# Eight layers on one core: the third attention's head outputs by channel, the fourth attention as a pipeline, and pieces of work moved between stages

## The chip, the core and the metric

The kernel runs on one core of one Trainium2 chip. Time is device microseconds of one execution, the median of several runs. A core has five engines with an instruction stream each, which meet through semaphores: PE (TensorE: matmuls and transposes; its weight loads are listed apart as PEld), DVE (VectorE), ACT (ScalarE), POOL (GpSimd) and SP (SyncE, which here issues DMAs). Results of PE land in PSUM and are read from there by DVE or ACT; everything else lies in SBUF. An engine executes its own instructions in order.

## The reference, cut to what matters

Sixteen batches (16 x 128 tokens x 256 channels, float32) go through eight layers: four cross-attentions, each followed by a feed-forward. Each layer works on a layernorm of x and adds its result to x.

```python
x = x + L0_xattn(ln(x), ctx, pos, ...)     # 32 heads of 8, rotary positions
x = x + L0_ffn(ln(x), ...)                 # product-key experts
x = x + L1_xattn(ln(x), ctx, mask, ...)    # 16 heads of 128
x = x + L1_ffn(ln(x), ...)                 # 7 routed experts (top 2) and a shared one
x = x + L2_xattn(ln(x), ctx, ...)
x = x + L2_ffn(ln(x), ...)                 # ternary weights
x = x + L3_xattn(ln(x), ctx, ...)
x = x + L3_ffn(ln(x), ...)                 # weights and activations rounded to fp8 by blocks of 32
```

The two attentions that the change rebuilds:

```python
def L2_xattn(x, y, ...):                    # 16 heads of 16; y has 128 tokens
    y_main, y_dca = y[:, :112], y[:, 112:]
    q     = _ln(x @ Wq + bq) * qn_w + qn_b          # each head by itself
    k     = _ln(y_main @ Wk + bk) * kn_w + kn_b;            v     = y_main @ Wv + bv
    k_dca = _ln(y_dca @ Wkd + bkd) * kn_dca_w + kn_dca_b;   v_dca = y_dca @ Wvd + bvd
    o = softmax(q k^T * 0.25) v + softmax(q k_dca^T * 0.25) v_dca     # two softmaxes
    return o @ Wo + bo

def L3_xattn(x, y, ...):                    # 16 heads of 128
    q, k, v = rmsnorm(x @ Wq, gq), rmsnorm(y @ Wk, gk), y @ Wv
    return (softmax(q k^T / sqrt(128)) v) @ Wo
```

## The kernel before, in words

`run` (L1610) goes through the plan of seven weight blocks and the eight stages in turn; weights of a later stage are loaded on SP while earlier ones compute. x stays in SBUF, one 128x256 tile for each batch. All matmuls are float32, and one matmul is two passes (two instructions) on PE in the trace. The order in which a stage's Python code emits work is the base of each engine's order; a scheduler may move an instruction within its queue, `high_priority` draws it forward, and `issue_after(i)` keeps a piece of work behind instruction i.

**Start.** `setup` loads x of two batches on SP, and positions, constants, context and `rows` (biases spread over the partitions) on ACT's queue; `run` then issues the first weights and the other x on SP. In `l0_attn` the work is `inputs` (layernorm and transposes of four batches), `front`, `turn`, `start` (scores and exponentials, `l0_terms`), `l0_heads`, `l0_norm`, `l0_out`; `inputs(1)` is held behind the last rotary multiply of `front(1)`. `l0_heads` packs four heads in 32-column tiles of PE (L356).

**First feed-forward** (`l0_ffn`). In batch b, behind the weights of each half, the `units` of batch b+1 are computed, two pieces for each half.

**Second feed-forward** (`l1_ffn`). Tokens are sorted into blocks of 128 rows for each expert; a loop over t does the stages of the blocks (fetch, unit, gate, down) as a pipeline. `shared(bs)` is the shared expert for a group of batches, a generator whose pieces are drawn forward by `next`. After the loop come `l2_inputs(0)`, `shared(groups[2])` and further `l2_inputs`. `l2_inputs(g)` gathers two routed results for each of two batches (`combine`, by indirect DMA on POOL's queue, then two DVE multiply-adds each, L1007), and makes the layernorm and transposes of them.

**Third attention** (`l2_attn`, L1062). For a batch, `front` makes q, k and v by matmuls, adds biases (DVE L1099, L1101), squares (ACT), reduces and takes the inverse root (DVE), then POOL multiplies by it (L1108), by the norm's weight (L1110), adds its bias (L1111), and writes v twice into `vx`, times the mask of main tokens and of the 16 others (L1115), beside columns of ones for the sums. `turn` transposes q and k (PE), copies them (ACT L1127) and spreads k over a block diagonal `kbd` (POOL L1130). For each half c of the heads: `l2_terms` makes the scores (PE L1173) in one PSUM buffer of two banks, the two maxima and subtractions (DVE L1182, L1184; 112 and 16 keys), and the exponential (ACT L1187). `l2_heads` transposes the exponentials (PE L184 `pT`), copies them (ACT L1198) and multiplies by `vx` in 64-column tiles, so that po has rows of outputs and sums for each head (PE L1202); ACT copies po to `u` (L1207). `l2_norm` transposes `u` back to tokens by channels (`pu`), takes the reciprocals of 16 sums for each token (DVE L1215) and multiplies (two L1217). `l2_out` transposes the sum of both softmaxes (L1227 `poT`), copies it (ACT L1229), adds `bo` to x on POOL (L1230), multiplies by Wo (PE L1233) and adds to x (DVE L1234). The loop keeps scores half a batch ahead, `turn` two batches ahead, `front` three.

**Fourth attention** (`l3_attn`). Batches go in groups of two. `project(g)` is a generator in six pieces: keys (PE `pk` L1386, POOL `kt` L1398, transposes `pkT`), queries (PE `pq` L1426, DVE `q` L1429), sums of squares (`pssq` L1433) and scales. For each batch and each r of four sets of four heads: scores S (PE L1472), maximum and scale (DVE L1474, L1475), four exponentials with sums (ACT L1479), reciprocal (DVE L1483), normalisation (POOL L1484), then a piece of the next group's `project`, then transposes `pT`, copy `eT` (DVE L1488), `po` (PE L1490), copy `oT` (DVE or ACT in turns), and `py` (PE L1498). One step's work is emitted whole before the next step's. With a group, one sixth of the last weights is rounded (`quantize`, 32 blocks).

**Last feed-forward** (`l3_ffn`). `quantize` rounds 1024 columns: maximum, scale, reciprocal and multiply on DVE, two adds (L1520, L1521) on the engine that the caller names (DVE for weights, POOL for x and h), and a multiply on POOL (L1522).

Of the kernel before, what the change touches and what calls it, by code (L numbers as in the profile page):

```python
# [34 lines left out]
for _name, _w in (  # L35
    ("bout0", 256), ("br", 8), ("gbias", 8), ("bq2", 256), ("bo2", 256), ("qn_w", 16), ("qn_b", 16),
    ("bkv_main", 512), ("bkv_dca", 512), ("kn_w", 16), ("kn_b", 16), ("knd_w", 16), ("knd_b", 16),
):
    ROWS[_name] = (_n, _w)
    _n += _w  # L40
# [12 lines left out]
class Net:  # L53
# [15 lines left out]
    def setup(self):  # L69
# [15 lines left out]
        nc.scalar.dma_start(out=self.rows, in_=a["rows"][0:NALL].partition_broadcast(P))  # L85
        nc.scalar.dma_start(out=self.ctxT[:, 2:B], in_=ctxT[:, 2:B])
        self.gains = cp.tile([P, 2], F32, tag="gains", name="gains")
        nc.scalar.dma_start(out=self.gains, in_=a["gains"])
# [129 lines left out]
    def l0_attn(self, w):  # L218
# [6 lines left out]
        with ExitStack() as es:  # L225
# [20 lines left out]
            def front(b):  # L246
# [15 lines left out]
                for k in range(2):  # L262
                    last = nc.vector.tensor_tensor(
                        by_head(t)[:, :, :, k], src[:, :, :, 1 - k], bc(self.sinT[:, b, :, k], 1, 64), ALU.mult
                    )
# [4 lines left out]
                return last  # L270
# [22 lines left out]
            last = front(1)  # L293
# [3 lines left out]
            with tc.issue_after(last.ins):  # L297
                inputs(1)
# [20 lines left out]
    def l0_terms(self, sp, kp, sc, b, c, qkT, kbd):  # L319
# [12 lines left out]
        for k in range(2):  # L332
# [3 lines left out]
            nc.vector.tensor_tensor(E[:, two], S[:, two], bc(mx, 3, P), ALU.subtract)  # L336
# [47 lines left out]
    def l0_ffn(self, w):  # L384
# [6 lines left out]
        with ExitStack() as es:  # L391
# [45 lines left out]
            sh = [units(0, q) for q in range(4)]  # L437
            for b in range(self.nb):
                more = b + 1 < self.nb
                nxt, after = [], None  # L440
                for half in range(2):
# [10 lines left out]
                    if more:  # L452
# [387 lines left out]
    def l1_ffn(self, w, after, ctx):  # L840
# [5 lines left out]
        with ExitStack() as es:  # L846
# [130 lines left out]
            rounding = self.ternary(sp, mm, after[:, 2048:])  # L977
            for t in range(NBLK + 2):
# [9 lines left out]
                if t > 10:  # L988
                    next(rounding, None)
            for _ in rounding:  # L990
                pass
            for g, bs in enumerate(groups[2:]):
                self.l2_inputs(g, tr)
# [18 lines left out]
    def l2_setup(self, ctx, w):  # L1012
# [10 lines left out]
        nc.gpsimd.tensor_copy(cd[:, :, 112:P], self.ctxT[:, :, 112:P])  # L1023

        bqk = op.tile([P, 32, 16], F32, tag="bqk", name="bqk")
        bv = op.tile([P, 256], F32, tag="bv", name="bv")
        nw = op.tile([P, 2, 16], F32, tag="nw", name="nw")
        nbi = op.tile([P, 2, 16], F32, tag="nbi", name="nbi")
        flat = bqk.rearrange("p h d -> p (h d)")
        for t, main, dca, skip, n in (  # L1030
            (flat[:, 256:512], "bkv_main", "bkv_dca", 0, 256), (bv, "bkv_main", "bkv_dca", 256, 256),
            (nw[:, 1, :], "kn_w", "knd_w", 0, 16), (nbi[:, 1, :], "kn_b", "knd_b", 0, 16),
        ):
            for name, part in ((main, slice(0, 112)), (dca, slice(112, P))):
                at = ROWS[name][0] + skip
                nc.scalar.dma_start(
                    out=t[part], in_=self.a["rows"][at : at + n].partition_broadcast(part.stop - part.start)
                )
        nc.vector.tensor_copy(flat[:, 0:256], self.row("bq2"))
        nc.vector.tensor_copy(nw[:, 0, :], self.row("qn_w"))  # L1040
        nc.vector.tensor_copy(nbi[:, 0, :], self.row("qn_b"))
# [7 lines left out]
        self.l2_const = cd, flat, bv, nw, nbi  # L1049
# [12 lines left out]
    def l2_attn(self, w):  # L1062
# [4 lines left out]
        Wo = w[:, 1536:2048].rearrange("p (c n) -> p c n", c=2)  # L1067
        with ExitStack() as es:
# [4 lines left out]
            tr = es.enter_context(tc.tile_pool(name="l2tr", bufs=2, space=PSUM))  # L1073
            pvp = es.enter_context(tc.tile_pool(name="l2pv", bufs=2, space=PSUM))
            cd, flat, bv, nw, nbi = self.l2_const

            vp = es.enter_context(tc.tile_pool(name="l2v", bufs=1))
            vx = [vp.tile([P, 16, 2, 32], F32, tag=f"vx{k}", name=f"vx{k}") for k in range(3)]
            for t in vx:
                for s in range(2):  # L1080
                    nc.scalar.copy(t[:, :, s, :], self.consts[:, 16 + s : 17 + s].unsqueeze(2).to_broadcast([P, 16, 32]))
# [708 lines left out]
```

## Time and profile before

| | us |
|---|---|
| runs (3) | 2538.73, 2539.52, 2540.11; median 2539.52 |
| profiled execution | 2537.55, its span 2535.8 |

| stretch of the span (us) | stage | length | PE busy | DVE busy | ACT busy | POOL busy |
|---|---|---|---|---|---|---|
| 13 to 291 | first attention | 278 | 247.6 | 206.8 | 172.0 | 68.2 |
| 296 to 714 | first feed-forward | 418 | 398.7 | 349.2 | 220.8 | 166.1 |
| 714 to 1147 | second attention | 433 | 409.6 | 239.8 | 168.3 | 109.2 |
| 1155 to 1365 | second feed-forward | 210 | 197.2 | 135.2 | 57.6 | 35.8 |
| 1365 to 1395 | third attention up to its first scores | 30 | 17.0 | 21.3 | 6.3 | 21.4 |
| 1395 to 1643 | third attention | 248 | 209.4 | 168.1 | 110.0 | 107.6 |
| 1650 to 1777 | third feed-forward | 127 | 127.0 | 32.7 | 17.1 | 3.6 |
| 1778 to 2317 | fourth attention | 539 | 509.3 | 336.1 | 285.2 | 148.9 |
| 2321 to 2536 | last feed-forward | 215 | 192.8 | 153.5 | 44.1 | 136.9 |

The second table is the view of busy time by stretch. A stretch whose length is close to PE's busy time is bound by PE; where no engine comes near the length, the time lies in waits of one engine for another. Rows of instructions, where they are shown below, give line, engine and operation, out<-in with shapes, the count, then busy time and the mean ns of one, then the idle time before them and who ended it.

### The profile page before, as it was taken

How to read it: one execution, taken by the hardware profiler on the slowest of the kernel's cores; microseconds unless marked ns; L12 is line 12 of the kernel's file. 1: busy time of each engine (PE TensorE's matmuls, PEld its weight loads, DVE VectorE, ACT ScalarE, POOL GpSimd, SP SyncE). 2: the span in 40 equal slices, each digit the busy share in tenths (PEclk: the TensorE clock that was granted, in tenths of full speed). 3: DMA queues.
4: the chain of work that ended last, by engine and by line, in shares of the span. 5: the costliest groups of instructions: out<-in, count | busy, mean ns of one | idle time of the engine just before them, and what ended most of it. 6: DMA issues, size and time to landing. Idle time of an engine off the chain costs nothing.

```text
span 2535.8 us, 37146 instructions
## 1 busy us (share of the span) xinstructions
PE 2320.0 (91%) x13628; PEld 1708.8 (67%) x13628; DVE 1665.5 (66%) x3884; ACT 1088.4 (43%) x2848; POOL 811.8 (32%) x736
## 2 busy tenths in 40 slices
PE   6999799999999999998997888799899999998798
PEld 3555589899977777775874455455576666665465
DVE  7777588888855555555666776532556666657964
ACT  4666555454524333441331444411555555554121
POOL 3222234343412222231007554200212222224765
PEclk8999899999999999999997899999999999999899
DMA  9000200000020000002224000000100000000000
GB/s 368 17 2 1 84 1 1 1 1 1 3 118 8 12 10 10 14 13 86 79 67 158 1 1 1 1 1 0 68 1 1 1 1 1 1 1 1 7 13 15
DMA packets 29845, 74.18 MB, mean 29 GB/s; under 512 B 6864, under 2 KB 21464, under 8 KB 24032
## 3 DMA queue, kind: packets, MB, share of 16 engines
q1 hardware_dynamic: 24768, 60.48, 6.4%
q0 software_dynamic: 3072, 8.39, 0.9%
q10 hardware_dynamic: 1824, 2.94, 0.3%
q8 instruction: 109, 1.79, 0.3%
q14 instruction: 72, 0.59, 0.1%
HBM read 45.84 MB, written 25.95 MB: 28 GB/s over the span
## 4 chain that ended last, share of the span: by engine, by line
PE 65%; DVE 21%; ACT 6%; POOL 4%; issue 4%; DMA 1%; POOLq 0%; ACTq 0%; DVEq 0%; SPq 0%
PE pT L184 5%; DVE g L519 5%; PE r L533 4%; PE py L669 4%; PE pt L608 4%; PE py L1498 3%; PE p L1315 3%; PE po L653 2%; PE fh L427 2%; PE fy L546 2%; PE py L1589 2%; PE pq L1426 2%; PE py L1323 2%; PE pg L1576 2%; PE pu L1576 2%
## 5 line engine op out<-in xcount | busy, mean ns | idle before, releaser
L184 PE MATMUL pT<-ident,E 128*128 128x128 f32 x1280 | 203.2, 285 | 45.1 <-POOL E L1484 11.9
L184 PEld LDWEIGHTS pT<-ident,E 128*128 128x128 f32 x1280 | 147.1, 145 | 100.9 <-issue 26.5
L509 POOL TENSOR_TENSOR g<-sim 128x1024 f32<-128x1024 f32 x64 | 140.5, 2215 | 217.6 <-ACT sim L474 183.0
L519 DVE SCALAR_TENSOR_TENSOR g<-g,th 128x1024 f32<-128x1024 f32 x128 | 194.6, 1580 | 0.0
L515 ACT ACTIVATE g<-sim 128x128 f32<-128x128 f32 x512 | 159.8, 391 | 33.5 <-PE r L533 32.9
L634 ACT ACTIVATE E<-E,mx 128x128 f32<-128x128 f32 x256 | 99.5, 390 | 160.0 <-DVE mx L631 138.6
L1479 ACT ACTIVATE E<-S,mx,sc 128x128 f32<-128x128 f32 x256 | 113.9, 458 | 83.3 <-DVE mx L1475 82.3
L1484 POOL TENSOR_TENSOR E<-E,rs 128x512 f32<-128x512 f32 x64 | 66.6, 1041 | 236.2 <-DVE rs L1483 106.0
L533 PE MATMUL r<-ident,g 128*128 128x128 f32 x1024 | 123.4, 275 | 18.6 <-DVE g L519 18.5
L669 PE MATMUL py<-w_w_l,oT 128*128 128x256 f32 x512 | 128.2, 383 | 5.3 <-DVE x L671 3.7
L533 PEld LDWEIGHTS r<-ident,g 128*128 128x128 f32 x1024 | 114.4, 142 | 26.4 <-DVE g L519 17.5
L1426 PE MATMUL pq<-xnT,w_w_l 128*128 128x256 f32 x512 | 126.7, 384 | 3.5 <-ACT sqk L1392 1.7
L639 POOL TENSOR_TENSOR E<-E,rs 128x512 f32<-128x512 f32 x64 | 66.6, 1041 | 194.7 <-DVE rs L638 144.8
L1498 PE MATMUL py<-w_w_l,oT 128*128 128x256 f32 x512 | 125.8, 387 | 3.1 <-DVE oT L65 2.9
L608 PE MATMUL pt<-xnT,w_w_l 128*128 128x256 f32 x512 | 121.1, 382 | 0.0
L427 PE MATMUL fh<-xnT,w_w_f 128*128 128x128 f32 x1024 | 121.0, 277 | 0.0
L669 PEld LDWEIGHTS py<-w_w_l,oT 128*128 128x128 f32 x512 | 93.9, 190 | 39.7 <-issue 20.4
L546 PE MATMUL fy<-w_w_f,wT 128*128 128x256 f32 x512 | 118.3, 379 | 0.0
L427 PEld LDWEIGHTS fh<-xnT,w_w_f 128*128 128x128 f32 x1024 | 116.7, 192 | 1.9
L1426 PEld LDWEIGHTS pq<-xnT,w_w_l 128*128 128x128 f32 x512 | 94.7, 191 | 28.6 <-issue 12.3
L1498 PEld LDWEIGHTS py<-w_w_l,oT 128*128 128x128 f32 x512 | 92.8, 190 | 29.1 <-DVE oT L65 11.6
L608 PEld LDWEIGHTS pt<-xnT,w_w_l 128*128 128x128 f32 x512 | 95.0, 192 | 15.2 <-issue 2.5
(403 smaller groups left out, 5561.6 us busy)
## 6 DMA issues: line engine op xcount, KB each, us to landing
w_w_f<-in_w_f SPq DMA_DIRECT2D x14, 1024.0 KB, 11.8
sent<-zero SPq DMA_DIRECT2D x14, 1024.0 KB, 20.6
w_w_l<-in_w_l SPq DMA_DIRECT2D x14, 1024.0 KB, 10.3
xb<-sent SPq DMA_DIRECT2D x38, 128.0 KB, 2.0
back<-yb SPq DMA_DIRECT2D x38, 128.0 KB, 1.8
x<-in_x SPq DMA_DIRECT2D x16, 128.0 KB, 2.9
out<-x SPq DMA_DIRECT2D x16, 128.0 KB, 1.7
ctx<-in_ctx ACTq DMA_DIRECT2D x1, 1024.0 KB, 8.0
```

The costliest lines, as they stand in the source:

```text
L184: self.nc.tensor.transpose(ps[:, i, :], src(i), self.ident)
L427: nc.tensor.matmul(ps[:, k, :], down[:, c, a * P : (a + 1) * P], xT[:, c, :], start=c == 0, stop=c == 1)
L509: nc.gpsimd.tensor_tensor(g, bc(sim[:, 2 * h, 8 * half : 8 * half + 8], 2, P), bc(sim[:, 2 * h + 1, :], 1, 8), ALU.add)
L515: nc.scalar.activation(g[:, k, :], sim[:, 2 * h + 1, :], AF.Identity, bias=sim[:, 2 * h, a : a + 1])
L519: nc.vector.scalar_tensor_tensor(gf, gf, th[:, h : h + 1], gf, ALU.is_ge, ALU.mult)
L533: nc.tensor.matmul(ps[:, k, :], G[h][:, 4 * q + k, :], self.ident, start=h == 0, stop=h == 3, is_transpose=True)
L546: self.nc.tensor.matmul(py, wT[:, k, :], up[:, a, :], start=a == 0, stop=a == 15)
L608: nc.tensor.matmul(ps[:, k], A[:, h + k, c, :], xT[:, c, :], start=c == 0, stop=c == 1)
L669: nc.tensor.matmul(pys[b], oT[:, j, :], Wo[:, h, :], start=h == 0, stop=h == 15)
L1426: nc.tensor.matmul(ps[:, l], Wq[:, c, h * P : (h + 1) * P], xT[:, c, :], start=c == 0, stop=c == 1)
L1479: nc.scalar.activation(E[:, j, :], S[:, j, :], AF.Exp, bias=mx[:, j : j + 1], scale=sc[:, i, 0, r, j : j + 1], accum_out=rs[:, j : j + 1],)
L1498: nc.tensor.matmul(py, oT[:, j, :], Wo[:, h, :], start=h == 0, stop=h == 15)
```

## The change

**Third attention.** The norm weights and biases are now a 128x6 table by channel, and three ACT activations with scale and bias in place of the one copy of the transposed q and k apply them; POOL's two passes go. v is added to its bias by one DVE instruction of 512 columns straight into `vx`, main and other tokens from two matmuls whose unused rows are zero (the 16 other tokens' columns of `ctxT` are zeroed in `l2_setup`, and put back from `cd` at the stage's end, both on POOL). `po` now holds outputs by channel in one half and, in the other, the sums spread over the same channels, by matmuls with `own` (ones) in place of `vx`; four heads lie side by side in 32-column tiles. DVE takes the reciprocal of all 128x256 sums and multiplies, which gives `oT` directly: `l2_norm`, its transposes, `u`, `poT` and the copies go. Wo's rows are laid out twice (w_l2 grows by 512 columns), so that the product with Wo adds both softmaxes in four matmuls for two. The transposes' PSUM pool has three buffers for two, `po` one for two. `front(2)` and `l2_inputs(1)` come after the first scores.

```diff
-                v = sp.tile([P, 256], F32, tag="v", name=f"v{b}", bufs=2)
-                nc.vector.tensor_tensor(v, pv, bv, ALU.add)
+                t = vx[b % 3]
+                last = nc.vector.tensor_tensor(
+                    t.rearrange("p h s d -> p s h d"), pv.rearrange("p s (h d) -> p s h d", h=16),
+                    bv.rearrange("p s (h d) -> p s h d", h=16), ALU.add,
+                )
...
                 nc.gpsimd.tensor_tensor(qk, qk, bc(r, 2, 16), ALU.mult)
-                nc.gpsimd.tensor_tensor(qk4, qk4, bc(nw, 2, 16), ALU.mult)
-                nc.gpsimd.tensor_tensor(qk4, qk4, bc(nbi, 2, 16), ALU.add)
-                for s in range(2):
-                    nc.gpsimd.tensor_tensor(
-                        t[:, :, s, 0:16], v3, self.consts[:, 16 + s : 17 + s].unsqueeze(2).to_broadcast([P, 16, 16]), ALU.mult
-                    )
...
-                nc.scalar.copy(qkT, ps)
+                for k, blocks, tok in ((0, slice(0, 2), slice(0, P)), (2, slice(2, 4), slice(0, 112)), (4, slice(2, 4), slice(112, P))):
+                    nc.scalar.activation(
+                        qkT[:, blocks, tok], ps[:, blocks, tok], AF.Identity, bias=norms[:, k + 1 : k + 2], scale=norms[:, k : k + 1]
+                    )
...
             front(0)
-            front(1)
-            front(2)
+            last = front(1)
...
             start(0, 0)
+            with tc.issue_after(last.ins):
+                self.l2_inputs(1, tr)
+            front(2)
...
-        for h in range(8):
-            i = h % 2
-            nc.tensor.matmul(
-                po[64 * i : 64 * i + 64, h // 2, :], vx[:, 8 * c + h].rearrange("p s d -> p (s d)"),
-                eTs[h // 4][:, h % 4, :], start=True, stop=True,
-            )
-        u = sp.tile([P, 4, P], F32, tag="u", name=f"u{b}_{c}", bufs=2)
-        nc.scalar.copy(u, po)
-        return u
+        for j in range(2):
+            for of in range(2):
+                for i in range(4):
+                    stand = own if of else vx[:, 8 * c + 4 * j + i]
+                    nc.tensor.matmul(
+                        po[32 * i : 32 * i + 32, of, j, :], stand.rearrange("p s d -> p (s d)"), eTs[j][:, i, :],
+                        start=True, stop=True,
+                    )
+        rz = sp.tile([P, 2, P], F32, tag="rz", name=f"rz{b}_{c}", bufs=2)
+        nc.vector.reciprocal(rz, po[:, 1])
+        nc.vector.tensor_tensor(oT[:, 2 * c : 2 * c + 2], po[:, 0], rz, ALU.mult)
...
-        for c in range(2):
-            nc.tensor.matmul(py, oT[:, c, :], Wo[:, c, :], start=c == 0, stop=c == 1)
+        for g in range(4):
+            nc.tensor.matmul(py, oT[:, g, :], Wo[:, g, :], start=g == 0, stop=g == 3)
```

**Seams.** `rows`, the rest of the context and `gains` are loaded on SP, among and behind the x loads, in place of ACT's queue. In `l0_attn` the second `inputs` is held behind the second subtraction of the first scores (`l0_last`) and no longer behind `front(1)`. In `l0_ffn` the first two `units` of batch 1 are made before the loop. In `l1_ffn` the shared expert of the last group is drawn forward in every second of the loop's last steps, and `l2_inputs(1)` has gone to the third attention.

```diff
             for t in range(NBLK + 2):
...
+                if t == NBLK - 6:
+                    late = shared(groups[2]) if len(groups) > 2 else late
+                if t % 2 == 0:
+                    next(late, None)
...
-            for g, bs in enumerate(groups[2:]):
-                self.l2_inputs(g, tr)
+            self.l2_inputs(0, tr)
+            for bs in groups[3:]:
                 for _ in shared(bs):
                     pass
```

**Fourth attention.** The steps (batch and r) are one sequence t. `terms(t)` is the old code from S to the normalised E, `turned(t)` the transposes and eT, `heads(t)` po and oT, `out(t)` the product with Wo. The rounding of the last weights goes in twelve pieces of 512 columns, one at every fourth step from the eighth.

```diff
+            terms(0)
+            terms(1)
+            more = iter(())
+            for t in range(len(steps)):
+                gi = t // 8
+                if t % 8 == 0:
+                    more = project(gi + 1) if gi + 1 < len(groups) else iter(())
+                if t % 8 == 6:
+                    for _ in more:
+                        pass
+                terms(t + 2)
+                eT = turned(t)
+                next(more, None)
+                heads(t, eT)
+                if t:
+                    last = out(t - 1)
+                piece = t // 4 - 2
+                if t % 4 == 0 and 0 <= piece < 12:
                     with tc.issue_after(last.ins):
-                        self.quantize(sp, self.w_f3[:, (gi - 1) * 1024 : gi * 1024], 32, "w", nc.vector)
+                        self.quantize(sp, self.w_f3[:, piece * 512 : (piece + 1) * 512], 16, "w", nc.vector)
+            out(len(steps) - 1)
```

**Last feed-forward.** py shares the transposes' PSUM pool, which has three buffers for two. The two adds of `quantize` are made on DVE for the first x group and for h of batches 0 and 1.

```diff
-                self.quantize(sp, xn.rearrange("p b d -> p (b d)"), 8 * n, "x", nc.gpsimd)
+                self.quantize(sp, xn.rearrange("p b d -> p (b d)"), 8 * n, "x", nc.gpsimd if g else nc.vector)
...
-                self.quantize(sp, hs[b], 32, "h", nc.gpsimd)
+                self.quantize(sp, hs[b], 32, "h", nc.vector if b < 2 else nc.gpsimd)
```

## The prediction

> **What bounds the kernel now.** I read three views in this order: the page's totals and chain, the busy time of each engine by stretch, then the groups of instructions of the stretches that the change touches.
>
> ```profile
> PE 2320.0 (91%) x13628; PEld 1708.8 (67%) x13628; DVE 1665.5 (66%) x3884; ACT 1088.4 (43%) x2848; POOL 811.8 (32%) x736
> ...
> PE 65%; DVE 21%; ACT 6%; POOL 4%; issue 4%; DMA 1%; POOLq 0%; ACTq 0%; DVEq 0%; SPq 0%
> ```
>
> PE is busy 91% of the span and is 65% of the chain: only the remaining 216 us, and PE work that is removed, can be won. The next view shows where PE stands idle (length, then busy time and instruction count of PE, PEld, DVE, ACT, POOL, PE's clock, DMA share, GB/s).
>
> ```profile
> 310.00:330.00 20.00, 16.27 (x113) 14.77 (x114) 15.61 (x29) 10.13 (x31) 4.74 (x3) 0.83 0.00 1
> 1324.60:1344.60 20.00, 14.40 (x47) 8.65 (x46) 11.34 (x29) 2.32 (x4) 15.43 (x19) 0.87 0.26 79
> 1365.00:1395.00 30.00, 16.96 (x56) 12.10 (x54) 21.30 (x65) 6.31 (x11) 21.43 (x26) 0.78 0.67 258
> 1457.43:1488.26 30.83, 26.66 (x182) 17.21 (x181) 21.99 (x65) 13.92 (x24) 15.75 (x19) 1.00 0.01 2
> 1820.00:1840.00 20.00, 16.06 (x67) 9.83 (x66) 12.47 (x48) 11.12 (x29) 6.68 (x6) 0.91 0.00 0
> 2104.00:2170.00 66.00, 63.65 (x342) 45.70 (x343) 41.19 (x107) 34.84 (x101) 19.32 (x16) 1.00 0.00 1
> 2296.00:2317.00 21.00, 16.23 (x81) 11.85 (x79) 14.24 (x37) 6.14 (x21) 6.63 (x8) 1.00 0.00 0
> ```
>
> The third attention (1365 to 1643) is the loosest stage. Two of its batches take 30.83 us, 15.4 each; per batch PE is busy 13.3, DVE 11.0, ACT 7.0, POOL 7.9. No engine is full: the wait runs round from scores to maximum to exponential to transpose. The fourth attention (1778 to 2317) is the opposite: 96% PE inside a group, loose only at its head (1820) and tail (2296).
>
> **Third attention, per batch.** The rows that price it (busy, mean ns):
>
> ```profile
> L1202 PE MATMUL po<-eT,vx 128*64 128x128 f32 x512 | 43.8, 294 | 0.4
> ...
> L1111 POOL TENSOR_TENSOR qk<-qk,nbi 128x512 f32<-128x512 f32 x15 | 19.2, 1282 | 0.9
> ...
> L1207 ACT COPY u<-po 128x512 f32<-128x512 f32 x32 | 18.7, 584 | 33.6 <-PE po L1202 33.6
> ...
> L1217 DVE TENSOR_TENSOR o<-pu,rs 128x128 f32<-128x128 f32 x64 | 16.4, 282 | 0.2
> ...
> L1115 POOL TENSOR_TENSOR vx<-v,consts 128x256 f32<-128x256 f32 x26 | 15.4, 613 | 4.7 <-PE po L1202 4.7
> ...
> L1215 DVE RECIPROCAL rs<-pu 128x16 f32<-128x16 f32 x32 | 8.1, 252 | 6.6 <-PE pu L184 6.5
> ...
> L1229 ACT COPY oT<-poT 128x256 f32<-128x256 f32 x16 | 6.0, 377 | 2.0 <-PE poT L1227 1.9
> ```
>
> POOL loses L1110 and L1111 (2 x 1.28) and two vx multiplies (2 x 0.61): -3.8 us. ACT loses two u copies (2 x 0.58) and oT (0.38) and gains two more, smaller pieces of the qkT copy (about +0.4): -1.1. PE passes of 128, 256 and 512 columns start 0.109, 0.217 and 0.43 us apart in the timeline. PE loses 8 pu passes (-0.87) and 4 poT passes (-0.44) and gains 4 py passes of 256 (+0.87). For po, four heads in 64-column tiles took 0.59 us; the first attention's 32-column tiles (L356) take 0.27 for four heads and some 0.2 to the next transpose. Eight such sets and two changes of shape, 2.5, against four of 0.59, 2.4: +0.1. PE in sum: -0.3.
>
> DVE gains, and here the change can turn. The new reciprocal covers 128x256, which no row shows. From below it is a 128x256 pass at 0.43 (x add, L1234). From above I extend the rows of 2, 4, 16 and 32 elements (155, 178, 251, 343 ns): the last step is 92 ns for 16, 5.8 ns each, so 0.34 + 224 x 0.0058 = 1.64. It lies nearest the long rows of its own operation, so I take 1.64. Two halves: 2 x (1.64 + 0.43 - 0.25 - 2 x 0.28) = +2.5; the value add doubles to 512 (0.69 for 0.42): +0.27. DVE goes from 11.0 to 13.8 and becomes the fullest engine; with the low bound it would be 11.4.
>
> The Trainium skill, page "VectorE: DVE Perf Modes", section "First, the fixed hardware budget", speaks against this part: the reciprocal is an iterative divide with a repeat count of 8. As an estimate from that and the page's 0.96 GHz, 256 elements would take 2.1 us instead of 1.64 and DVE 14.7 a batch. The rows' slope is under that, but they stop at 32 elements.
>
> Now the period. Behind the reciprocal on DVE wait, by the changed order, the x add, the multiply, then the next maximum and subtraction (1.09 + 0.26 + 1.09 + 0.28) that free the only score buffer; PE's next po also waits for the multiply, po having one buffer now. Against that, the round trips po to u to pu to o to poT to oT go. Walking one period by these durations I get 14.0 to 15.0. I take 14.8: -0.6 over 14 periods, -8. Ends: DVE packed, 13.8, -22; DVE queue late, 16.1, +10. Its prologue (1365 to 1395, 30 us to the first scores) waits for gathers behind a weight load, 386 GB/s in that stretch:
>
> ```profile
> 1364.02 6.01 DMA moe_y<-back,slot
> ...
> 1370.89 6.82 DMA moe_y<-back,slot
> ```
>
> The second inputs and the third front now come after the first scores, so the second wait is off the path, but DVE's 21.3 us are mostly only pushed on: -5 (-14 to +2). The zeroing and restoring of 16 columns on POOL lies in its slack.
>
> **Seams.** At the start ACT waits 9.6 us for rows behind its own DMA issues; they move to SP, past the x loads. The next inputs no longer hold DVE before the first exponential (PE was busy 5.90 of 20 to 30 us). -6 (-10 to -1; if the later context load holds the third front it is the -1). First feed-forward: two unit pieces fill part of the 3.7 us at 310 to 330: -2 (-3.7 to 0). The second feed-forward's shared expert for the last group, 20 us alone with PE 14.4, goes into the last four even steps of the block loop: PE loses 5.6 idle and 1.9 of slow clock (0.13 x 14.4), of which the loop's own queues take something: -6 (-10 to +3).
>
> **Fourth attention.** In a group of two batches PE must issue: pq and py 64 passes each at 0.217 (27.8), S, pT and pkT 128 at 0.109 (14.0), po and pk 32 at 0.43 (13.8), sums and small ones some 2.9: 58.5. x adds are 64.3 us apart from group to group. Issuing S two steps ahead, with a projection piece between pT and po and py one step late, hides the E, eT and oT waits. What the row shows idle is 2.35 of 66; I take that, 2.3 for each of seven groups: -16 (0 to -40, all 5.8). The last group has no projection to hide behind, 40.0 us; a step's PE work is S 0.87, pT 0.44, po 0.86, py 1.74, 3.9 x 8 = 31: -7 (0 to -9). Head: PE idles 3.9 at 1820: -2 (0 to -5). Twelve half pieces of weight rounding are the same DVE elements plus some 0.1 us of start each, under PE. Together -25 (-50 to 0).
>
> **Last feed-forward.**
>
> ```profile
> 2343.00:2356.00 13.00, 5.01 (x16) 3.03 (x15) 12.97 (x12) 1.47 (x3) 10.50 (x7) 0.75 0.00 0
> 2370.00:2390.00 20.00, 13.53 (x47) 9.04 (x48) 19.66 (x15) 2.80 (x6) 15.71 (x7) 0.83 0.04 14
> ```
>
> Three pairs of POOL adds (2.35 and 2.40) become DVE adds at 1.22: 2.3 us less latency each, where PE idles 8.0 and 6.5. But DVE is full there, so the gain is only the difference: -3 (-10 to +4).
>
> **Sum.** -6 - 2 - 6 - 5 - 8 - 25 - 3 = -55. Profiled execution 2537.55 (span 2535.8 and 1.75 around it): 2482.5. The median of the runs is 2.0 above that execution: 2484.5, said as 2485.
>
> **Rivals.** (1) The fourth attention is PE-bound already: its steady 16 us don't come, since its row has PE at 96% and what is idle may be PE's own changes of tile shape, and the seams give half of their 14. Then 2485 + 16 + 7 = 2508. Against it: the S, pT, po waits are named E and eT in the groups' idle time. (2) DVE's queue becomes the third attention's bound: reciprocal and multiply (2.07) stand ahead of the maximum and subtraction (2.72), and with one po buffer PE waits both out in each half. If 2.4 us a half don't overlap, the period is 15.1 + 4.8 = 19.9, +4.5 x 14 = +63 in place of -8: 2485 + 71 = 2556. It decides from a period of 18.8, where +47 eats the other -47. For it: 13.8 of DVE work in one queue; against it: the longest single wait of PE on DVE in the stage is 2.5 us now, and ACT and POOL get shorter. (3) Both loops pack fully: 13.8 a batch (-14 more) and half of the other 3.5 us a group (-12): 2485 - 26 = 2459.
>
> **Chances.** Forecast 0.52, rival 1 0.20, rival 2 0.11, rival 3 0.17. The time is the forecast's, 2485. The range takes in rivals 1 and 3 with the single terms' ends, 2446 to 2525; rival 2's upper part stays out. A measurement of this kernel can tell about 0.2% (5 us) from no change. Only rival 2 and a tail of rival 1 don't win: faster 0.87, same 0.03, slower 0.10.
>
> **What would show it.** After: L1210 near 1.64 us and DVE near 92% in the third attention with 14.8 between its x adds; if L1210 is above 3 us or the adds are over 18.8 apart, rival 2. x adds of the fourth attention 62 apart by group, 31 to 33 for the last. First scores of the third attention 5 us sooner after the block loop's end, no 20 us stretch of shared expert alone. I am wrong if PE waits show DVE rz or oT as the largest releaser, or if the projection pieces leave E late.

## The result, and the profile after

The changed kernel takes 2505.46 us (median of 4 runs, 2499.38 to 2511.41) against 2539.82 us; ratio 0.9863, 95% interval 0.9832 to 0.9895. A second measurement, on the chip of the first experiments, gave 2503.22 us (5 runs, 2498.58 to 2513.85), ratio 0.9851, interval 0.9828 to 0.9874. By the ratios it is faster by 35 to 38 us; by the medians, 2539.82 and 2545.46 before, by 34 and 42. Faster was forecast, and the time lies within the forecast's range, but the gain is two thirds of the 55 us in the sum.

The first fence holds the page's totals of the changed kernel; the second its busy time by stage, with the columns of the views before (length, busy time and count of PE, PEld, DVE, ACT, POOL, then PE's clock, DMA share, GB/s).

```profile
span 2508.3 us, 37903 instructions
...
PE 2283.9 (91%) x14012; PEld 1703.1 (68%) x14012; DVE 1704.1 (68%) x3904; ACT 1067.1 (43%) x2826; POOL 745.6 (30%) x676
```

```profile
294.20:716.00 421.80, 401.22 (x3115) 374.82 (x3116) 349.11 (x693) 220.82 (x633) 166.88 (x115) 0.98 0.03 11
...
1157.40:1368.00 210.60, 198.37 (x890) 144.66 (x890) 121.36 (x318) 57.24 (x167) 14.27 (x18) 0.94 0.20 64
...
1400.00:1634.50 234.50, 190.67 (x1774) 126.36 (x1772) 216.04 (x479) 94.53 (x158) 74.66 (x85) 0.95 0.03 10
...
1769.60:2293.10 523.50, 495.25 (x2648) 367.98 (x2649) 345.75 (x950) 281.35 (x814) 149.10 (x129) 0.99 0.02 9
2297.20:2508.30 211.10, 189.54 (x684) 116.99 (x684) 150.67 (x192) 43.85 (x78) 128.54 (x62) 0.98 0.03 11
```

The fourth attention is 15 us shorter (538.7 before), the last feed-forward 3.6. The first feed-forward is 3 us longer (418.7 before), and the second has the length it had (210.7). In the third attention DVE, which was busy 168 of 248 us, is now busy 216 of 234.5. Two stretches inside that stage, two quiet batches and two into which the inputs of later ones fall:

```profile
1426.30:1453.40 27.10, 23.66 (x230) 15.73 (x230) 26.89 (x63) 12.45 (x21) 6.21 (x6) 1.00 0.01 2
...
1514.30:1548.10 33.80, 25.14 (x226) 17.01 (x219) 30.12 (x74) 11.94 (x20) 12.51 (x14) 0.90 0.06 16
```

In the quiet ones DVE is busy 26.89 of 27.10 us: its queue is the period, 13.5 us a batch where it was 15.4 over two batches before. With inputs it is 16.9, and there DVE has idle time again. The groups of the stage show what filled it:

```profile
L1210 DVE RECIPROCAL rz<-po 128x256 f32<-128x256 f32 x32 | 55.8, 1745 | 2.0 <-PE po L1205 1.9
L1185 DVE TENSOR_TENSOR E<-S,mx 128x896 f32<-128x896 f32 x31 | 33.4, 1077 | 0.0
L1183 DVE TENSOR_REDUCE mx<-S 128x8 f32<-128x896 f32 x31 | 33.3, 1076 | 3.9 <-PE S L1174 3.9
```

The new reciprocal is the stage's largest piece of work on any engine, 1.745 us each, and DVE hardly idles ahead of it (2.0 us in 32). DVE's wait for scores, the longest in the stage before, has nearly gone; before, then after (who waited <- for whom: us in total, times, longest):

```profile
DVE mx L1182 <- PE S L1173: 26.9, 17, 4.3
```

```profile
DVE mx L1183 <- PE S L1174: 3.9, 3, 2.9
```

PE's longest waits there are now for the layernorm of later inputs and for q and k, not for the reciprocal's product oT:

```profile
PE pxT L168 <- DVE xn L154: 11.4, 2, 5.7
PE pqkT L181 <- POOL qk L1115: 5.8, 6, 1.7
...
PE py L1219 <- DVE oT L1211: 2.6, 3, 1.3
```

### The profile page after: what moved, and what is told of

It is laid out like the page before. It is cut to its first block, busy times and chain, and to the rows that moved or that the text cites. A ratio compares the mean times of both kernels' runs of the same rounds, so it can differ in the third digit from the quotient of the medians.

```text
span 2508.3 us, 37903 instructions
## 1 busy us (share of the span) xinstructions
PE 2283.9 (91%) x14012; PEld 1703.1 (68%) x14012; DVE 1704.1 (68%) x3904; ACT 1067.1 (43%) x2826; POOL 745.6 (30%) x676
## 5 line engine op out<-in xcount | busy, mean ns | idle before, releaser
L181 PE MATMUL pT<-ident,E 128*128 128x128 f32 x1280 | 197.5, 284 | 13.6 <-POOL E L637 8.9
L181 PEld LDWEIGHTS pT<-ident,E 128*128 128x128 f32 x1280 | 147.7, 145 | 49.9 <-issue 19.5
L531 PEld LDWEIGHTS r<-ident,g 128*128 128x128 f32 x1024 | 115.4, 142 | 27.7 <-DVE g L517 17.5
L667 PE MATMUL py<-w_w_l,oT 128*128 128x256 f32 x512 | 129.1, 385 | 5.2 <-DVE x L669 3.6
L1498 PE MATMUL py<-w_w_l,oT 128*128 128x256 f32 x512 | 131.2, 383 | 0.1
L1412 PE MATMUL pq<-xnT,w_w_l 128*128 128x256 f32 x512 | 116.2, 380 | 1.0 <-ACT xnT L67 0.6
L1412 PEld LDWEIGHTS pq<-xnT,w_w_l 128*128 128x128 f32 x512 | 94.9, 190 | 14.3 <-ACT sqk L1378 1.2
```

Of the source, the lines that this page charges most:

```text
L181: self.nc.tensor.transpose(ps[:, i, :], src(i), self.ident)
L531: nc.tensor.matmul(ps[:, k, :], G[h][:, 4 * q + k, :], self.ident, start=h == 0, stop=h == 3, is_transpose=True)
L667: nc.tensor.matmul(pys[b], oT[:, j, :], Wo[:, h, :], start=h == 0, stop=h == 15)
L1412: nc.tensor.matmul(ps[:, l], Wq[:, c, h * P : (h + 1) * P], xT[:, c, :], start=c == 0, stop=c == 1)
L1498: nc.tensor.matmul(pys[b], oT[:, j, :], Wo[:, h, :], start=h == 0, stop=h == 15)
```

## The experiments

All are the changed kernel with one thing altered, but for the two that name several. Medians are compared through the ratio to the kernel before on the same chip.

**The changed kernel again.**

> The changed kernel once more. Its four times lie between 2499 and 2511 us, 12 us apart, where those of the kernel before lie within 3.5. Theory A: the spread sits between the end of the second attention and the first block of the second feed-forward's loop, which took 45.2 us in the profile after (PE clock 0.69 and 0.50 there) and 37.1 before; then this profile, if its span is near 2499, shows that stretch at about 37 and the rest as before. Theory B: the spread sits in DVE's queue of the third attention (266.5 us in the profile after); then that stage differs by some 10 us between the two profiles and the other stretch does not.

Span 2498.3. The stretch from the router's last matmul to the loop's first block took 40.6 us, not 45.1, with a higher clock; the two fences are the same stretch in the first profile and in this one.

```profile
1145.00:1205.00 60.00, 50.49 (x152) 28.63 (x150) 29.90 (x108) 6.93 (x13) 8.13 (x13) 0.77 0.25 85
```

```profile
1145.00:1205.00 60.00, 50.47 (x173) 29.82 (x173) 31.39 (x112) 8.95 (x19) 8.17 (x13) 0.86 0.27 90
```

PE is busy equally long and does 152 instructions in one and 173 in the other: what differs is the granted clock, 0.77 and 0.86. Of the 10 us between the profiles 4.5 lie here, 2.4 in the third attention's first batch. From 1171 to 1179 us four passes of pd take 2.08 us in the first profile and 1.13 in the second. The times of the nine runs follow their mean clock, but for one pair, from 2498.58 at 0.977 to 2513.85 at 0.969. The kernel before spreads as widely when it is run more often: on the chip of the run with the power on POOL its 17 times go from 2537.53 at 0.975 to 2549.66 at 0.969. So theory A holds in part: this stretch has 4.5 of the 10 us, and it took 40.6 where the theory said 37. All the profiles of the changed kernel and its variants have 40 to 45 us there, the one of the kernel before 37.0. Some of that difference is no matter of the clock: in every one of those profiles PE waits 3.0 us for DVE's `oh` ahead of the block table's bias, 1.9 us before.

**The seams undone.**

```diff
+        nc.scalar.dma_start(out=self.rows, in_=a["rows"][0:NALL].partition_broadcast(P))
+        nc.scalar.dma_start(out=self.ctxT[:, 2:B], in_=ctxT[:, 2:B])
...
-            with tc.issue_after(self.l0_last.ins):
+            with tc.issue_after(last.ins):
...
-            first = [units(1, q) for q in range(2)] if self.nb > 1 else []
+            first = []
...
-                if t == NBLK - 6:
-                    late = shared(groups[2]) if len(groups) > 2 else late
```

> The changed kernel with the seams as before: rows, context and gains again on ACT's queue, the second inputs of the first attention behind front(1), no unit pieces before the first feed-forward's loop, the shared expert of the third group after the block loop. Theory A (the block loop with the shared group inside saves 8 us by itself, 144.7 + 20.7 against 130.3 + 43.3, and the start 1.5): slower than the changed kernel by 8 to 12 us, about 2515. Theory B (seams give nothing, as the sum of the stages up to 1368 us says: 2.6 us later than before): within 3 us of the changed kernel.

2506.98 us, ratio 0.9846 (0.983 to 0.9863): no difference from the changed kernel that the runs can tell (3.8 us slower by the medians, 1 us faster by the ratios). The profile takes it apart: the first attention ends 5 us later (294.4), the first feed-forward is 3 us shorter (419.0), and from the loop's first block to the third attention it takes 167.3 us against 163.7 to 165.3. The first of these says little, since the kernel before, with the same start, ended that stage at 290.9, and the profiles that have the changed start end it anywhere from 288.4 to 291.8. The kernel before needed 173.5 from the first block to the third attention; the other 6 us come from `l2_inputs(1)` having left this stretch, which theory A had credited to the shared expert.

**The third attention's column tiles undone** (64-column tiles, copy u, transposes pu and poT, two products with Wo, and the PSUM pools of before).

```diff
-        rz = sp.tile([P, 2, P], F32, tag="rz", name=f"rz{b}_{c}", bufs=2)
-        nc.vector.reciprocal(rz, po[:, 1])
-        nc.vector.tensor_tensor(oT[:, 2 * c : 2 * c + 2], po[:, 0], rz, ALU.mult)
+        u = sp.tile([P, 4, P], F32, tag="u", name=f"u{b}_{c}", bufs=2)
+        nc.scalar.copy(u, po)
```

> The changed kernel with head outputs and sums of the third attention as before: 64-column tiles, ACT's copy u, transposes pu and poT, two products with Wo; the norm weights stay in ACT's activations and v in one add. Theory A (DVE became the bound: 26.9 of 27.1 us busy in two batches, 1.745 us for each reciprocal of 128x256): what the tiles save on PE and ACT goes back on DVE, so without them the stage is at most 6 us longer or even shorter, total within 6 us of the changed kernel. Theory B (the tiles are what shortened the stage): the period goes back to 15.4 us, the stage to some 275 us, total 8 to 12 us slower.

2513.27 us, ratio 0.9875 (0.9857 to 0.9893) and 274.9 us for the stage against 264.5 and 266.5: theory B by its numbers. But the x adds say where: from the first product pqk to the first x add 64.1 us against 55.8 and 58.4, and from the first x add to the last 210.8 against 208.3 to 208.8. The tiles shorten the way through the first batch by 6 to 8 us, and the 15 periods that follow by 2. The period did not go back to theory B's 15.4: the mean of the first twelve is 15.0 us here, and 15.0 and 15.1 with the new tiles. What the tiles take from PE and ACT in the steady part they give to DVE, as theory A had it.

**The reciprocal cut down.**

```diff
-        nc.vector.reciprocal(rz, po[:, 1])
-        nc.vector.tensor_tensor(oT[:, 2 * c : 2 * c + 2], po[:, 0], rz, ALU.mult)
+        nc.vector.reciprocal(rz[:, :, 0:8], po[:, 1, :, 0:8])
+        nc.vector.tensor_tensor(oT[:, 2 * c : 2 * c + 2], po[:, 0], bc(self.ones, 1, 2), ALU.mult)
```

> The changed kernel; left out: of the third attention's 256 columns of sums only 16 are turned into reciprocals, and the product is with a constant, so the outputs are not normalised. It takes 1.5 us from DVE for each half, 3.0 a batch, and leaves everything else. Theory A (DVE sets the period since the change): quiet batches go from 13.45 to about 12 us, where PE's 11.8 bounds them, those with inputs from 15.8 to 13 to 14; the stage is 20 to 35 us shorter than the 264.5 to 266.5 of the changed kernel. Theory B (the wait runs round the engines, as it did before the change with DVE 71% busy): the stage is at most 10 us shorter.

2474.91 us, ratio 0.973 (0.9705 to 0.9754); the stage takes 231.7 us, 33 less. The same 190 us of the stage, first in the changed kernel (second profile), then in this one:

```profile
1410.00:1600.00 190.00, 157.86 (x1458) 106.63 (x1461) 178.42 (x414) 79.56 (x135) 60.45 (x68) 0.96 0.03 8
```

```profile
1410.00:1600.00 190.00, 172.73 (x1672) 115.55 (x1671) 160.74 (x458) 89.76 (x151) 66.52 (x74) 0.97 0.03 8
```

DVE falls from 178 to 161 although more batches pass, and PE rises from 158 to 173. Theory A is shown: since the change the reciprocal on DVE sets the period, and of the 48 us that the wide reciprocals add (3.0 a batch), 33 lengthen the stage. The run shortens DVE's queue and the way from po to oT at once, and po has one buffer; that it is the queue rests on the 26.89 of 27.10 us of the quiet batches. It agrees with the Trainium skill, page "TensorEngine Tiling (Array Packing)", section "PSUM Bottleneck", which says that tiling speeds up TensorE but not the evacuation of PSUM, and advises to use both ScalarE and VectorE for it: here the change took ACT's copies away and gave DVE all 512 columns of po.

**DVE relieved through POOL, twice.** First the inverse root as one power on POOL:

```diff
-                r = self.rsqrt(sp, r, 32, "r", b)
+                nc.gpsimd.tensor_tensor(r, r, self.mhalf.to_broadcast([P, 32]), ALU.pow)
```

> The changed kernel; in the third attention the inverse root of the 32 variances of a token is one POOL power (the form that the layernorms use, 0.73 us for two columns) in place of eleven small DVE instructions of 0.15 to 0.55 us, some 1.9 us of DVE a batch. Theory A (DVE is what sets the third attention's period: 13.45 us in quiet batches with DVE 99% busy, 15.8 where the next inputs come in): the x adds draw together by 1 to 2 us a batch and the stage ends 10 to 25 us sooner. Theory B (the wait runs round the engines and DVE is busy beside it): the longer way over POOL delays q and k; stage within 5 us, or longer.

2537.21 us, ratio 0.9984: nearly the whole gain was gone, stage 297.6 us. The reason is a price that neither theory had:

```profile
L1114 POOL TENSOR_TENSOR r<-r,mhalf 128x32 f32<-128x32 f32 x14 | 76.4, 5456 | 25.1 <-DVE r L1113 25.0
...
L120 POOL TENSOR_TENSOR rs<-rs,mhalf 128x2 f32<-128x2 f32 x6 | 4.2, 700 | 0.4
```

The power's cost grows with the columns, 5.5 us for 32 and 0.7 for 2, and POOL's queue became the way of q and k: PE waits 30.9 us for them, 5.8 in the changed kernel. It says nothing on DVE; the run above does. The second attempt is the last experiment. The reverse, the layernorm's root moved from POOL to DVE, with the two bad seams undone:

> The changed kernel with the second inputs of the first attention held behind front(1) and no unit pieces ahead of the first feed-forward's loop (the version that was 5 us faster than the changed kernel), and in the third attention the inverse root of the layernorm on DVE (thirteen small instructions) in place of POOL, on which DVE waited 9.7 us in five waits. Theory A (the wait is longer than the instructions, 2 to 3 us against 1.6): the stage 3 to 8 us shorter than 264.5, total near 2493. Theory B (on a full DVE more instructions only make the queue longer): the stage 0 to 8 us longer, total 2498 or more.

2506.78 us, ratio 0.985 (0.983 to 0.9869), stage 268.2 us against 264.2 without it: theory B. Thirteen small instructions on a full queue cost more than the waits that they replaced.

**The gathers behind the first kbd.** In the changed kernel POOL's queue ran so (start, us, what, idle before):

```profile
1377.92 1.00 POOL L1007 DMA_INDIRECT moe_y<-back,slot  x1 [14.79 <-DVE r_y L128]
1379.22 0.97 POOL L1007 DMA_INDIRECT moe_y<-back,slot  x1 [0.31 <-DVE r_t L131]
1380.50 0.95 POOL L1007 DMA_INDIRECT moe_y<-back,slot  x1 [0.30 <-DVE r_y L133]
1381.75 0.95 POOL L1007 DMA_INDIRECT moe_y<-back,slot  x1 [0.30 <-issue]
1382.72 1.06 POOL L1115 TENSOR_TENSOR qk<-qk,r_y 128x512 f32<-128x512 f32 x1
```

The multiply that PE waits for (8.8 us) stands behind four gathers for later batches. In the experiment `turn` returns its last kbd, and the inputs are held behind that.

```diff
-            last = front(1)
+            front(1)
             turn(0)
-            turn(1)
+            last = turn(1)
```

> The changed kernel; the second inputs of the third attention (gathers on POOL's queue) are held behind the last kbd of the second turn, and no longer behind the second front. Theory A (four to eight gathers of about 1.25 us stood ahead of the multiply of q and k, L1115, on POOL, which started at 1382.7 us though its factors were there at 1378): first scores of the stage 5 to 8 us sooner after the first pqk, total 3 to 8 us faster than the changed kernel. Theory B (the gathers then come late and stall DVE at the third and fourth batch): the gain at the first scores is lost by the fourth x add, total within 3 us.

The first scores come 13.6 us after the first pqk and not 23.3, the first x add 49.9 and not 55.8 (second profile). The second x add then comes 23.2 us later where it was 13.2, and by the fourth the lead is a lag (99.3 against 96.0). 2510.26 us, ratio 0.9876 (0.9861 to 0.989): theory B; the stage is 4 to 6 us longer, and the total alone does not tell it from the changed kernel. So the gathers did cost 10 us ahead of the first scores, and they cost no less where they were moved to.

**The order within a step of the fourth attention.**

```diff
+                next(more, None)
                 terms(t + 2)
                 eT = turned(t)
-                next(more, None)
-                heads(t, eT)
                 if t:
                     last = out(t - 1)
+                heads(t, eT)
```

> The changed kernel; in a step of the fourth attention the projection piece is emitted first, and the product with Wo of the step before stands ahead of po. In the profile after, PE idled 2.8 us a group: po on the eT copy 1.1, the sums of squares on ACT's squares 1.3, keys 0.4. Theory A (PE's idle time moved from the old waits to these, and both are due to the order in the step): both waits go, 63.4 us a group becomes 61 to 62, the stage 10 to 16 us shorter. Theory B (what is idle returns at another place of the same in-order queue whatever the order, PE being 96% busy): 63.4 stays within 0.5, the total within 4 us.

2507.82 us, ratio 0.986; 63.3 to 63.6 us for four of the five groups of the steady part and 62.1 for the fifth, stage 524.4. Theory B: with py ahead of po, po still waits for eT (6.5 us in the five groups of the middle, 5.5 in the changed kernel), and the wait for the sums of squares only falls from 6.9 to 4.0.

**The weight rounding left out of the fourth attention.**

```diff
-                    with tc.issue_after(last.ins):
-                        self.quantize(sp, self.w_f3[:, piece * 512 : (piece + 1) * 512], 16, "w", nc.vector)
```

> The changed kernel; left out: the rounding of the last weights during the fourth attention (twelve pieces, some 5 us of DVE and 1 of POOL each), so the last feed-forward works on unrounded weights. Theory A (those pieces stand in DVE's queue ahead of the eT copies and the squares' neighbours, and PE's 2.8 idle us a group are waits for what they push back): 63.4 us a group becomes 61 to 62, the stage 10 to 16 us shorter than 523.5. Theory B (PE's own starts and the in-order queue set it): 63.4 stays within 0.5, the stage within 4 us.

2486.25 us, ratio 0.9779 (0.9755 to 0.9803); 60.4 us a group, stage 505.9. One group of the changed kernel, then one of this kernel:

```profile
2054.20:2117.50 63.30, 60.53 (x328) 45.00 (x327) 43.29 (x118) 34.54 (x101) 18.78 (x16) 1.00 0.00 1
```

```profile
2036.90:2097.50 60.60, 59.83 (x328) 44.91 (x327) 35.45 (x101) 34.35 (x101) 16.68 (x14) 1.00 0.00 1
```

PE does the same 328 instructions; its idle time goes from 2.8 to 0.8 us. DVE was busy 43 of 63 us only, but the rounding in the stage, 49 us of DVE and 12.5 of POOL, costs 17.7 us of its length. Theory A, by more than its numbers; in the middle of the stage po's wait for eT (5.5 us) is gone, and the wait for the sums of squares is 2.8 where it was 6.3 (second profile). The run takes out the DVE and the POOL part together, so it does not say which of the two costs it; that the eT copy is DVE's speaks for DVE.

**The fourth attention as before.**

> The changed kernel with the fourth attention's steps emitted whole as before, and the weight rounding in six pieces by group. Theory A (the pipeline gains at head and tail, 11 us, and little within a group, 63.4 against 64.3 us): 15 to 18 us slower than the changed kernel, about 2521, with 64.3 us from group to group and 66 us for the last. Theory B (part of the fourth attention's gain came from its neighbours): under 10 us slower.

2524.94 us, ratio 0.9913 (0.9894 to 0.9931), stage 538.8: 64.3 us a group again. The pipeline is worth 15 us of its stage and, by the ratios, 0.6% of the whole, some 16 us; the medians on this chip are 22 us apart. Theory A.

**Two seams undone.**

> The changed kernel with two of the seams undone: the second inputs of the first attention held behind front(1) again (the loads stay on SP), and no unit pieces ahead of the first feed-forward's loop. Theory A (the first moved a 3 us wait of PE from 22 to 28 us without shortening it; the second costs 3 us, 421.7 to 422.6 against 418.7 to 419.0 us): 4 to 7 us faster than the changed kernel, first feed-forward near 419. Theory B (both are neutral or good): same or slower.

2498.02 us (2495.72 to 2503.06), ratio 0.9833 (0.982 to 0.9846), the fastest version that leaves nothing out; the interval overlaps the changed kernel's, so the total alone doesn't prove the 5 us. The profiles do for one part: the first feed-forward takes 418.6 us, as it did before the change; all four profiles without the unit pieces have 418.6 to 419.0 there, all nine with them 421.7 to 422.6. The new hold is a wait that moved: with it, the first transposes pT came at 35.6 us and the first x add at 61.0, with the old one at 30.7 and 57.2; but the stage ends at 289.2 to 289.4 and 289.6.

**Everything together**, with the Newton steps on POOL and the rounding in 24 pieces.

> The changed kernel with the two seams undone that cost time (hold and unit pieces), the three Newton steps of the third attention's inverse root on POOL (twelve small instructions in place of nine on DVE, some 1.5 us of DVE a batch), and the weight rounding of the fourth attention in 24 pieces of 256 columns, each behind the eT copy of its step, in place of twelve of 512. Theory A (DVE's queue sets the third attention's period, and long runs of rounding ahead of eT cost the fourth 3 us a group): the third attention 10 to 20 us shorter than 264.2, the fourth 5 to 12 shorter than 523.5, total 2470 to 2485. Theory B (POOL's small instructions are slow enough that q and k come late, as with the power; the rounding's work and not its grouping costs): third attention as long or longer, fourth within 4 us, total 2495 or more.

2506.46 us, ratio 0.9843: theory B on both counts. The third attention took 269.4 us; PE now waits 15.9 us for q and k from POOL (5.9 in the run of two seams undone), where twelve instructions of 0.25 us stand ahead of the multiply. The fourth took 524.6. Smaller pieces of rounding behind the eT copies don't help: po's wait for eT is gone, but the wait for the sums of squares has grown from 6.9 to 15.1 us. It is the work, and not its grouping, and the idle time only changed its place.

## Why the prediction was right, and where it was too large

The direction, the range and the account of the third attention were right. But the time, 2505, is 20 us over the forecast's 2485 and nearly that of rival 1, 2508, and what rival 1 named came in large part: a middle group of the fourth attention gave 0.9 us and not 2.3, and the seams gave about half of their 14 (-5.5 and -7.7 us in the two profiles). Its reason did not come: PE was not at its own limit, as the run without the rounding shows (60.4 us a group). One term, the unit pieces, left its own range, and one stretch that got longer had no term.

The terms of the sum, against the two profiles (us; each from its first PE instruction or x add to that of the next):

| term | forecast | profile after | second profile |
|---|---|---|---|
| start, to the first feed-forward | -6 | -1.5 | -1.7 |
| first feed-forward and second attention | -2 | +4.1 | +3.7 |
| router to first block | no term | +8.1 | +3.6 |
| block loop to third attention | -6 | -8.1 | -9.7 |
| third attention, to its first x add | -5 | -4.7 | -7.3 |
| third attention, the rest | -8 | -6.1 | -5.6 |
| fourth attention | -25 | -15.6 | -15.5 |
| last feed-forward | -3 | -3.6 | -4.7 |
| sum (with small remainders) | -55 | -27.5 | -37.5 |

**Third attention: right, and by the mechanism named.** DVE did become the fullest engine, busy 92% of the stage as forecast: 13.45 us a batch in quiet batches and 15.1 in those with inputs (13.8 forecast for all). The mean of the first twelve periods is 15.0 us (14.8 forecast, 15.4 before), made of 13 to 14 in quiet batches and 16 to 17.5 with inputs. The forecast took 15.4 for 14 periods; the last three of the kernel before were 13.0, 9.5 and 7.5, so the mean of all 15 fell from 14.3 to 13.9. The reciprocal took 1.745 us where the rows gave 1.64; the estimate that the Trainium skill's iterative divide ("VectorE: DVE Perf Modes", "First, the fixed hardware budget") led to, 2.1, was further off. The rival with DVE as the bound had its mechanism but not its price: reciprocal and subtraction didn't add up on top of the old period, they replaced the old round trips, at about the same period (15.0 us with the old tiles too). The gain at the prologue came where it was forecast, ahead of the scores: 24.6 and 23.2 us from the first pqk to the first scores, 29.5 before. Yet the second wait for gathers was not off the path, since gathers still stand ahead of the first multiply on POOL. And the moved inputs cost again behind the scores: from there to the first x add the old tiles take 39.4 us, the kernel before 33.6; the new tiles, with fewer links, take 33.8 and 32.6.

**Fourth attention: the step that failed.** "Issuing S two steps ahead, with a projection piece between pT and po and py one step late, hides the E, eT and oT waits", priced at the 2.3 us idle in each of seven groups. The old waits did go, and new ones came, 15.0 us in sum where 11.7 had been. These are PE's waits in the middle of the stage (about five groups; us in total, times, longest), before and after:

```profile
PE pkT L184 <- POOL kt L1398: 4.5, 5, 0.9
PE pT L184 <- POOL E L1484: 3.2, 6, 0.5
PE py L1498 <- DVE oT L65: 1.7, 5, 0.3
PE po L1490 <- DVE eT L1488: 1.3, 5, 0.3
PE pq L1426 <- ACT sqk L1392: 1.0, 5, 0.2
```

```profile
PE pssq L1419 <- ACT w_w_l L1416: 6.9, 17, 0.6
PE po L1484 <- DVE eT L1478: 5.5, 5, 1.1
PE pk L1372 <- ACT E L1465: 2.6, 6, 0.4
```

A group went from 64.3 to 63.4 us only, and not by idle time: PE idles 2.8 us in it, 2.35 before, and its 328 instructions are busy for 60.5 us where they were for 62.05. The prediction had costed the rounding pieces at some 0.1 us of start each, "under PE"; the run without them shows that they are what the remaining idle time hangs on, 3.0 us a group. Head and tail came out at 11 us in sum (forecast 9), but not as described. The first x add comes 6.1 us later after the stage's start, with PE idle for 10.5 us up to it where it was 8.3 (the forecast had 2 less), and 2.2 us are lost between the last x add and the next stage. The last group takes 29.6 us for 39.9 (31 to 33 forecast), the group before it 59.3 for 65.8, and the second x add follows the first 2.7 us sooner. The five middle groups give 4.6; in all 15.6. With the steps emitted whole again the first x add is back at 89.8 us, so the shift belongs to the pipeline.

**Seams: two terms of the wrong sign or size.** The start gave the 3 us of an earlier first matmul, but the held inputs were transposed 2.6 us later (28.0 against 25.4 us), and the first x add came at 61.0 us against 58.7; 1.5 us were left at the stage's end, less than the spread of that end between profiles of the same code (288.4 to 291.8). The unit pieces ahead of the first loop filled no idle time that counted; without them the stage is 3 us shorter. The shared expert's term was right in size by luck: 6 of its 8 to 10 us belong to the inputs that left the stretch.

**Last feed-forward: right in size, not in place.** PE's longest wait, for POOL's h, was 8.0 us and is 8.6. The wait of py for the x add fell from 6.6 to 1.7, with py in a pool of three buffers, but waits for h and x on DVE of 3.2 and 1.3 us came in its place, and PE's waits in the stage are 18.7 and 18.3 us in sum. What fell is PE's busy time, 192.7 to 189.5 us for the same 684 instructions, with a clock of 0.98 where it was 0.95. No run undoes this stage, so its cause stays open.

**What no term had:** the stretch before the block loop, 3.6 to 8.1 us. The difference between the two profiles goes with the clock that the execution got; of what both profiles have over the kernel before, some 2 us are longer waits of PE for DVE there (`seen` 1.2 us, not among the waits before; `oh` 3.0 for 1.9).

**What stays open.** By runs that undo it, the pipeline of the fourth attention is worth 15 us and the third attention's tiles 6 to 10, and the seams nothing that can be told. The norm weights in ACT's activations, the single add of v and the moved inputs were not undone by themselves.

## What to carry to other kernels

Before a result is moved from a transposed to a channel layout, count the columns that the evacuating engine will then read: sixteen-fold sums made a reciprocal 1.5 us longer, and it sat on the engine that the same change had just made the bound. When a pipeline takes a wait from a nearly full in-order engine, ask which helper queue it will wait for next, and look there for filler work costed at nothing; leaving that filler out for one run prices it. A transfer or a filler piece moved forward is moved past everything else on its queue.

## What was not expected of the hardware

The time of a power on POOL grows with the columns: 0.7 us for 128x2, 5.46 for 128x32. The reciprocal's slope from 32 to 256 columns is 6.3 ns a column ((1745 - 343) / 224), above the 5.8 between 16 and 32. The granted clock of a run, 0.969 to 0.977, nearly orders the times of the same kernel over 15 us; of the 10 us between two profiles of it, 4.5 fall where PE waits a few us between the second attention and the block loop (0.77 and 0.86).
